# A recurrent layer on one core: the input product of two time-step pairs in seven products of halves

## The chip, the core and the metric

The kernel runs on one core of a Trainium2 chip. The core has a matrix engine (TensorE, PE in the profile), three engines for elementwise work (VectorE or DVE, ScalarE or ACT, GpSimd or POOL), and a queue engine (SyncE or SP) that issues nearly all transfers here. Each engine works through its own instructions in order and waits on semaphores for the others. Working memory is SBUF (128 partitions); TensorE writes into eight banks of PSUM, each 128 x 512 float32. The metric is the device time of one execution in microseconds, here the median of three runs.

## The reference, cut to what matters

The input x has 64 sequences of 256 time steps of 1024 numbers. Layer 0 is a recurrence:

```python
xW = jnp.einsum('ntd,dh->nth', x, Wx) + b
def step(prev_h, xw):
    next_h = jnp.tanh(prev_h @ Wh + xw)
    return next_h, next_h
_, h_t = jax.lax.scan(step, h0, swapaxes(xW, 0, 1))
x = x + swapaxes(h_t, 0, 1)
```

Layer 1 splits its input into sums and differences over time, multiplies all of them by one gate per sequence and channel, and puts them together again. Since the gate is the same for all of them, this is a multiplication of x by the gate, and with the residual x becomes x * (2 + gate) in all (the kernel's `factor`). The gate is sigmoid(silu(cond W1' + b1) W2' + b2).

So there are two large products: x Wx, which depends on nothing, over 16384 rows; and h Wh, 256 times one after the other with 64 rows.

## The kernel before

**Layout.** Two time steps are a pair (S = 2): 2 x 64 = 128 rows, which fill the array. There are NP = 128 pairs. A slab is a tile of 128 x 1024 float32, for a pair the transposed x.

**The product x Wx.** The precision wanted is that of float32[...]. Wx is split once into three parts, `wx_s[k][0..2]` (high bits, rest times 4096, and a mix of both), and so is x of each pair (class `XWork`): `high_bits` masks (L125, VectorE), `low` makes x1 = x - high (L302, VectorE), `difference` makes x2 (L307, VectorE), `cast` makes x0 (L313, ACT). `whole` then issues 48 matmuls of 128 x 128 by 128 x 512: 16 of x2 into two banks `mixed`, 16 of x1 and 16 of x0 into two banks `main` (L278). `take_mixed` takes `mixed` to SBUF (L323, ACT) and adds the bias (L324, GpSimd); `finish_half` adds `main` (L380, VectorE). The sum goes to DRAM (`store`, L390) and comes back in the layout of the h steps (`reload`, L403, eight transfers of 64 KB).

**The product h Wh.** It is a Strassen product in seven products of quarters: `StrassenWeight` holds the combinations of Wh, `strassen_sides` makes those of h (L229 to L232, four operations of 128 x 128 on VectorE, both inputs in SBUF), and `strassen_product` issues 16 small matmuls for each (L199). In the main loop the order of a step is 1, 4, 2, 5, 6, 7, 3. The quarters of the next h come off as soon as their products are there: an addition, tanh on ACT (L760), a transpose on VectorE (L764). `m5` and `m7` share the banks `main0` and `main1` with the x products.

**Stages.** The first ALONE = 12 steps run beside the loading and splitting of Wx, the gate's products and the x products of pairs 1 to 6. From step 12 on, the order on VectorE, ACT, GpSimd and SP is the program's (a manual schedule), as it is on TensorE all along. Steps come in groups of M = 2. After the second step of a group, `beside_x` issues the 48 matmuls of one pair, and around these, in this order on the other engines: the residual x + h (L623, VectorE), the scaling of finished steps by `factor` (`scale`, L505, GpSimd), the taking of `mixed`, the copies of the next step's xw into PSUM (`put_part`, L618, ACT), the split of the next pair, and the two finishes. These matmuls are what TensorE does while the last chain of the step (addition, tanh, transposes, sides) runs. I call this stretch a gap. Its sum is stored in the next group.

The outputs of the first steps, which came before `factor` was known, wait in DRAM (`kept`) and are scaled one per two gaps in `kept_step` (L732, GpSimd).

The additions of a step that matter below, in their order on VectorE:

```python
nc.vector.tensor_add(y[:, 3], m5, xw[:, 3])         # L786
transpose(0)
nc.vector.tensor_add(y[:, 3], y[:, 3], u)           # L799, u copied by ACT in L798
nc.vector.tensor_add(y[:, 2], accs[2], u)           # L800
for o in (3, 2):
    nc.vector.tensor_add(quad(h, o), m7, y[:, o])   # L804
```

## Time and profile before

| | us |
|---|---|
| median of three runs | 3045.84 (3045.01 to 3046.71) |
| the profiled execution, its own time | 3044.8 |
| its span, first to last instruction | 3043.0 |
| TensorE busy | 3033.8 |
| VectorE busy | 1797.0 |
| ScalarE busy | 871.0 |
| GpSimd busy | 844.4 |

300.59 MB were moved, 99 GB/s in the mean; the main queue took 27.5% of the 16 DMA engines' time. TensorE's granted clock was full throughout.

The profile is of one execution. Busy times are sums over an engine's instructions; since matmuls are pipelined and their ends modelled, a busy TensorE is one that had always an instruction under way. A line of the groups tells the line of the code, the engine and operation, the tiles out<-in, the shape, the count, then the busy time and the mean of one in ns, then the engine's idle time before such instructions and what ended it. The chain is followed back from the last instruction through what released each piece of work. A line of the timeline gives start, length, engine, line, and in brackets the idle time before.

### The profile page before, as it was taken

How to read it: one execution, taken by the hardware profiler on the slowest of the kernel's cores; microseconds unless marked ns; L12 is line 12 of the kernel's file. 1: busy time of each engine (PE TensorE's matmuls, PEld its weight loads, DVE VectorE, ACT ScalarE, POOL GpSimd, SP SyncE). 2: the span in 40 equal slices, each digit the busy share in tenths (PEclk: the TensorE clock that was granted, in tenths of full speed). 3: DMA queues.
4: the chain of work that ended last, by engine and by line, in shares of the span. 5: the costliest groups of instructions: out<-in, count | busy, mean ns of one | idle time of the engine just before them, and what ended most of it. 6: DMA issues, size and time to landing. Idle time of an engine off the chain costs nothing.

```text
span 3043.0 us, 144709 instructions
## 1 busy us (share of the span) xinstructions
PE 3033.8 (100%) x63862; PEld 2706.8 (89%) x63862; DVE 1797.0 (59%) x4928; ACT 871.0 (29%) x2641; POOL 844.4 (28%) x521
## 2 busy tenths in 40 slices
PE   9999999999999999999999999999999999999999
PEld 6888899889988898889888998899889988998888
DVE  8556555655555555555555565555655565565555
ACT  3222222222222222222222322232222222222222
POOL 2233333332223222322232223222222222222321
PEclk9999999999999999999999999999999999999999
DMA  7323323332222222222222222222222222222222
GB/s 264 123 90 115 101 100 100 109 107 86 86 101 98 86 86 99 100 86 86 96 99 89 86 93 97 95 86 89 102 95 86 86 102 97 86 86 102 97 86 76
DMA packets 164616, 300.59 MB, mean 99 GB/s; under 512 B 44192, under 2 KB 110496, under 8 KB 164000
## 3 DMA queue, kind: packets, MB, share of 16 engines
q1 hardware_dynamic: 163856, 290.81, 27.5%
q8 instruction: 514, 8.42, 1.1%
q14 instruction: 102, 0.84, 0.1%
q10 hardware_dynamic: 144, 0.52, 0.0%
HBM read 154.93 MB, written 136.31 MB: 96 GB/s over the span
## 4 chain that ended last, share of the span: by engine, by line
PE 98%; DMA 1%; POOL 0%; issue 0%; DVE 0%; SPq 0%; DVEq 0%; ACT 0%
PE main L278 30%; PE acc L199 22%; PE mixed L278 16%; PE m_h L199 15%; PE main_h L199 14%; PE m L199 1%; DMA h0T<-condT 0%; DMA wh<-wh 0%; DMA w<-w1T 0%; POOL sum L324 0%; PE gate_ps L216 0%; DMA x<-xT 0%; DMA b_row<-b 0%; DVE x L302 0%; SPq L134 0%
## 5 line engine op out<-in xcount | busy, mean ns | idle before, releaser
L278 PE MATMUL main<-wx,x 128*128 128x512 f32 x4064 | 945.7, 389 | 0.3 <-DVE x L302 0.3
L505 POOL TENSOR_TENSOR x<-x,factor 128x512 f32<-128x512 f32 x242 | 358.4, 1481 | 2030.8 <-issue 1177.2
L278 PEld LDWEIGHTS main<-wx,x 128*128 128x128 f32 x4064 | 762.0, 188 | 161.2 <-issue 2.2
L278 PE MATMUL mixed<-wx,x 128*128 128x512 f32 x2032 | 499.1, 397 | 0.0
L324 POOL TENSOR_TENSOR sum<-sum,b_row 128x512 f32<-128x512 f32 x254 | 448.1, 1784 | 50.6 <-DMA w<-w1T 43.2
L278 PEld LDWEIGHTS mixed<-wx,x 128*128 128x128 f32 x2032 | 371.7, 188 | 97.9 <-issue 24.8
L760 ACT ACTIVATE h<-h 128x128 f32<-128x128 f32 x976 | 275.7, 306 | 547.8 <-DVE h L784 330.9
L302 DVE TENSOR_TENSOR x<-x,x_high 128x1024 fp32r<-128x1024 f32 x127 | 171.1, 1347 | 253.6 <-PE main L278 253.5
L764 DVE STREAM_TRANSPOSE hT<-h 128x128 f32<-128x128 f32 x972 | 298.0, 307 | 38.2 <-ACT h L760 38.1
L380 DVE SCALAR_TENSOR_TENSOR sum<-main,sum 128x512 f32<-128x512 f32 x254 | 175.6, 691 | 206.2 <-PE main L278 204.5
L199 PE MATMUL acc<-wh,s 128*32 128x128 f32 x8160 | 270.8, 273 | 1.2 <-issue 1.2
L199 PE MATMUL acc<-t,hT 128*32 128x128 f32 x8160 | 270.9, 273 | 0.7 <-issue 0.7
L199 PE MATMUL acc<-wh,hT 128*32 128x128 f32 x8160 | 269.9, 273 | 0.0
L778 ACT COPY y<-m_h 128x128 f32<-128x128 f32 x244 | 65.0, 267 | 709.7 <-PE m_h L199 694.6
L199 PE MATMUL m_h<-wh,hT 128*32 128x128 f32 x7808 | 261.4, 274 | 0.3 <-issue 0.3
L199 PE MATMUL main_h<-t,s 128*32 128x128 f32 x7808 | 259.6, 273 | 0.0
L199 PE MATMUL m_h<-t,s 128*32 128x128 f32 x7808 | 258.8, 273 | 0.1
L199 PE MATMUL main_h<-wh,s 128*32 128x128 f32 x7808 | 258.6, 273 | 0.0
L199 PEld LDWEIGHTS m_h<-wh,hT 128*32 128x32 f32 x7808 | 208.6, 110 | 44.7 <-issue 44.7
L618 ACT COPY acc<-xw 128x128 f32<-128x128 f32 x732 | 177.8, 264 | 234.3 <-DMA xw<-sum_d 165.0
L323 ACT ACTIVATE sum<-mixed 128x512 f32<-128x512 f32 x254 | 152.0, 599 | 320.9 <-PE mixed L278 320.8
L307 DVE SCALAR_TENSOR_TENSOR x<-x_high,x 128x1024 fp32r<-128x1024 f32 x127 | 190.7, 1502 | 86.9 <-PE mixed L278 86.8
(81 smaller groups left out, 2931.7 us busy)
## 6 DMA issues: line engine op xcount, KB each, us to landing
x<-xT SPq DMA_DIRECT2D x127, 512.0 KB, 4.0
sum_d<-sum SPq DMA_DIRECT2D x127, 512.0 KB, 2.9
xw<-sum_d SPq DMA_DIRECT2D x1016, 64.0 KB, 2.0
yT<-x SPq DMA_DIRECT2D x122, 512.0 KB, 2.7
wh<-wh SPq DMA_DIRECT2D x8, 512.0 KB, 10.9
w<-w1T SPq DMA_DIRECT2D x8, 512.0 KB, 8.5
w<-w2T SPq DMA_DIRECT2D x8, 512.0 KB, 4.0
wx<-wx SPq DMA_DIRECT2D x7, 512.0 KB, 8.5
```

The lines of the kernel that those rows point to most:

```text
L199: nc.tensor.matmul(out=out[q * R : (q + 1) * R], lhsT=a[:, k * R : (k + 1) * R], rhs=wh_s.sides[i][k][:, q], start=first and k == 0, stop= ...
L278: nc.tensor.matmul(out=acc[h], lhsT=v[:, k * P : (k + 1) * P], rhs=wx_s[k][which][:, h * HALF : (h + 1) * HALF], start=start and k == 0, s ...
L302: nc.vector.tensor_sub(self.x1, x, self.high)
L307: nc.vector.scalar_tensor_tensor(out=self.x2, in0=self.high, scalar=1.0 + DOWN, in1=pairs[i], op0=ALU.mult, op1=ALU.subtract)
L323: nc.scalar.activation(s, self.mixed[h], AF.Copy, scale=-1.0)
L324: nc.gpsimd.tensor_add(s, s, b_row[:, h * HALF : (h + 1) * HALF])
L380: nc.vector.scalar_tensor_tensor(out=v, in0=self.main[h], scalar=1.0 + DOWN, in1=v, op0=ALU.mult, op1=ALU.add)
L505: nc.gpsimd.tensor_mul(of_step(x, s), of_step(x, s), blocks(factor))
L618: nc.scalar.copy(part, xws[t // S][t % S][:, j])
L760: nc.scalar.activation(quad(h, j), quad(h, j), AF.Tanh)
L764: nc.vector.transpose(quad(hT, j), quad(h, j))
L778: nc.scalar.copy(y[:, 0], m16)
```

## The change

The x product of pairs 16 to 127 is done for two pairs together. The 256 rows and 1024 columns of x, and Wx, are cut into quarters, and the product of the 2 x 2 quarters is made in seven products (Winograd's form of Strassen's) in place of eight. Each of the seven, a `Product`, is 12 matmuls of the same shape: four k blocks for each of x2, x1 and x0.

- **Units and chunks.** Two pairs are a unit; U = 4 units (eight pairs) are a chunk, and there are 13 of these, then one of 3 units and one of 1. Inside a chunk the products go by form (1, 2, 5, 6, 3, 7, 4), and for each form over the units.
- **Forms of Wx.** For each of the seven forms, the three parts of 128 x 2048 are made on chip and kept in DRAM (`forms_d`). Forms 1, 2 and 3 are pieces of `wx_s` and are stored during steps 2 to 10 (36 transfers of 256 KB). Forms 4 to 7 are combinations, made by `form_jobs` (GpSimd, VectorE, ACT) while the pairs 7 to 15 are multiplied in the old way, one right after another. Then the memory of the whole Wx is given up. In the main loop the three parts of a form (3 x 1 MB) are streamed in by `load_weights`, two forms ahead.
- **Forms of x.** `Form` splits a quarter of x, or a combination of quarters: a21 + a22 on VectorE for form 5, and others in place on GpSimd. These GpSimd operations, and those that add products up (`u` and `v`), are not issued where they arise but put on a list (`pool_later`), which is worked off in the first step after the gap.
- **The gap.** `beside_x` now issues 3 or 4 products (2 or 3 in the first chunk) instead of 48 matmuls. The finish of the last product and the mask and x2 of a split go into the first step after the gap, behind the copy of y0; x1 and x0 of that split go behind the copy of u, ahead of L799 (`slot`).
- **Other moves.** The two scalings of the pair before, the reload of xw and the loads of x move to the first step of a group, behind `slot`. x of a pair is read again from DRAM for the residual.

```diff
+FIRST = 16
+U = 4
+UNITS = [U] * 13 + [3, 1]
+FORMS = 3
+ORDER = (1, 2, 5, 6, 3, 7, 4)
...
+        for k in range(KB):
+            top, low = slab(f"top{k}"), slab(f"low{k}")
+            nc.sync.dma_start(out=top, in_=wx[k])
+            nc.sync.dma_start(out=low, in_=wx[KB + k])
+            l, r = cols(0), cols(1)
+            nc.gpsimd.tensor_sub(top[:, l], top[:, r], top[:, l])
+            nc.gpsimd.tensor_sub(top[:, r], low[:, r], top[:, r])
+            nc.gpsimd.tensor_sub(low[:, r], low[:, r], top[:, l])
+            nc.gpsimd.tensor_sub(low[:, l], low[:, l], low[:, r])
...
+            if self.p == 5:
+                self.src = forms.tile([P, HALF], F32, tag="s1", bufs=1, name=f"s1_{n}")
+                nc.vector.tensor_add(self.src, a[21], a[22])
+                self.later(lambda: (pool_sub(a[21], a[11], a[21]), pool_sub(a[11], a[22], a[21])))
...
+            if self.p == 6:
+                self.later(lambda: (pool_sub(a[12], a[12], a[11]), load_quarter(self.c + 1, self.v, 11)))
...
+        def first(self) -> None:
+            nc.vector.tensor_scalar(
+                out=self.high, in0=self.src[:].bitcast(I32), scalar1=HIGH, scalar2=None, op0=ALU.bitwise_and
+            )
+            nc.vector.scalar_tensor_tensor(
+                out=self.x2, in0=self.high, scalar=1.0 + DOWN, in1=self.src, op0=ALU.mult, op1=ALU.subtract
+            )
...
+        def second(self) -> None:
+            nc.vector.tensor_sub(self.x1, self.src, self.high)
+            nc.scalar.copy(self.x0, self.high)
...
+            one(self.mixed, f.x2, 2, True, True)
+            one(self.main, f.x1, 1, True, False)
+            one(self.main, f.x0, 0, False, True)
...
+            nc.scalar.activation(t, self.mixed, AF.Copy, scale=-1.0)
+            nc.gpsimd.tensor_add(t, t, add)
...
+            nc.vector.scalar_tensor_tensor(out=out, in0=self.main, scalar=1.0 + DOWN, in1=t, op0=ALU.mult, op1=ALU.add)
...
+            if p in (6, 7):
+                v = self.state("v")
+                when_h(self.c, lambda: (nc.gpsimd.tensor_add if p == 6 else nc.gpsimd.tensor_sub)(u, u, v))
...
         strassen_product(m16, sides[1], 1, True)
         nc.scalar.copy(y[:, 0], m16)
-        if t == first and coming is not None:
-            coming.cast()
+        if slot:
+            slot.pop(0)()
+        if s == 0 and i > ALONE // S and i - 1 in pairs and i < NP - 1:
+            scale(pairs[i - 1], 0)
+            scale(pairs[i - 1], 1)
+        if s == 0:
+            for f in pool_later:
+                f()
+            pool_later.clear()
+            if i + 1 < NP:
+                reload(i + 1)
+                load_x(i + 1)
...
         strassen_product(m16, sides[6], 6)
-        mark = nc.scalar.copy(u, m16)
+        nc.scalar.copy(u, m16)
+        if slot:
+            slot.pop(0)()
         nc.vector.tensor_add(y[:, 3], y[:, 3], u)
```

`beside_x` after the change:

```python
for j in range(n):
    m = done[0]
    u = Product(m, (n - 1 - j) % 2 ^ 1)
    u.multiply(n > 2 and j == n - 1)
    done[0] += 1
    if j == 0:
        residual(t, hT)
    if before and (before.c, before.v) == (u.c, u.v):
        before.finish()
        before = None
    u.take_mixed()
    if j == 0:
        accs[:] = [put_part(t + 1, o) for o in range(3)]
    if before:
        before.finish()
    before = u
    if last_of_product(m):
        load_weights(u.m + 2)
    if j + 1 < n:
        prepare()
slot.append(lambda: (before.finish(), prepare(True)))
```

## The prediction

> **What bounds the kernel now.** I read the busy shares first, then the chain that ended last, then the groups, then the timeline of one period of 23.47 us, and last the timeline of a stretch where VectorE and GpSimd meet. The page:

> ```profile
> span 3043.0 us, 144709 instructions
> PE 3033.8 (100%) x63862; PEld 2706.8 (89%) x63862; DVE 1797.0 (59%) x4928; ACT 871.0 (29%) x2641; POOL 844.4 (28%) x521
> PE 98%; DMA 1%; POOL 0%; issue 0%; DVE 0%; SPq 0%; DVEq 0%; ACT 0%
> ...
> L278 PE MATMUL main<-wx,x 128*128 128x512 f32 x4064 | 945.7, 389 | 0.3 <-DVE x L302 0.3
> L505 POOL TENSOR_TENSOR x<-x,factor 128x512 f32<-128x512 f32 x242 | 358.4, 1481 | 2030.8 <-issue 1177.2
> L324 POOL TENSOR_TENSOR sum<-sum,b_row 128x512 f32<-128x512 f32 x254 | 448.1, 1784 | 50.6 <-DMA w<-w1T 43.2
> ```

> TensorE alone sets the time; everything else is cover. The 389 ns of a matmul overlap, so its price comes from the chain in order of time:

> ```profile
> 185.05 7.25 PE main L278 x32
> ```

> 7.25/32 = 0.2266 us each. A pair costs 48 of them, 10.88 us; two h steps of 6.13 us and about 0.3 us at the seam fill up the 23.47.

> How much room do the other engines have inside a step? This is the timeline of the end of the first step of a group, which began at 1507.34 (T0 below):

> ```profile
> 1511.98 0.27 ACT L798 COPY u<-m_h 128x128 f32<-128x128 f32 x1 [0.88 <-PE m_h L199]
> 1512.28 0.29 DVE L799 TENSOR_TENSOR y<-y,u 128x128 f32<-128x128 f32 x1 [0.66 <-ACT u L798]
> 1512.49 0.28 DVE L800 TENSOR_TENSOR y<-acc,u 128x128 f32<-128x128 f32 x1
> 1512.86 0.49 DVE L804 TENSOR_TENSOR h<-main_h,y 128x128 f32<-128x128 f32 x2
> 1513.52 0.31 DVE L764 STREAM_TRANSPOSE hT<-h 128x128 f32<-128x128 f32 x1
> ...
> 1514.24 0.89 PEld L199 LDWEIGHTS acc<-t,hT 128*32 128x32 f32 x32
> ```

> The addition y3 += u (L799) starts at T0+4.94 and ends at T0+5.23; through L800, L804 and tanh it leads to the transpose that ends at 1513.83, and the second product of the next step loads that quarter at 1514.24. The slack is 0.41 us there, and 0.09 more before L804: 0.5 us. If L799 is later than that, TensorE waits.

> What can make it late is seen before the main loop (VectorE's and GpSimd's timelines):

> ```profile
> 132.35 1.38 DVE L230 TENSOR_TENSOR s<-hT 128x128 f32<-128x128 f32 x1
> 133.65 1.37 DVE L231 TENSOR_TENSOR s<-s,hT 128x128 f32<-128x128 f32 x1
> ...
> 132.18 1.39 POOL L568 TENSOR_TENSOR x<-x,hT 128x512 f32<-128x512 f32 x1 [10.56 <-DVE hT L520]
> 133.54 2.62 POOL L324 TENSOR_TENSOR sum<-sum,b_row 128x512 f32<-128x512 f32 x2
> ```

> Operations that take 0.28 us elsewhere take 1.38: each ends about 0.16 us after a GpSimd operation. The two engines take turns.

> [...] The trace agrees, with the 1.38 us above, and with L786 (one input from PSUM), which took 0.29 us at 1517.22 beside a GpSimd operation that ran from 1516.35 to 1517.64. [...] between about 4 and 26 us the DMA view shows 400 to 420 GB/s, and TensorE's matmuls waited on "issue" in four places and 1.9 us over the whole span: its instructions arrive beside full transfers.

> From these places I take as held time: 1.15 us for a GpSimd 128x512 operation (1.30 alone, less the part that overlaps), 0.55 for a VectorE two-input 128x512 one (0.69), 0.30 for the 128x512 bit mask (half of L125's 0.687, less overlap), 0.15 for a 128x128 one.

> **The change, part by part.**

> *Products removed.* Pairs 7 to 127 cost 121 x 48 = 5808 matmuls in the main part. Now pairs 7 to 15 cost 432 and 56 units of two pairs cost 56 x 7 x 12 = 4704, together 5136. 672 x 0.2266 = 152 us less. Loads of the array keep their shape (188 ns, under 226). This is the whole gain.

> *Forms of Wx (pairs 7 to 15 in a row).* The plain products hide 10.88 us of other work per pair. Every second pair loads two slabs, but their loads stand on SP behind the stores of the forms before, which wait for ACT (about 5.7 us into the pair), then 4 us landing and three GpSimd subtractions to about 15.1, then VectorE's subtraction, x1 (L302) and the first finish (L380), to about 18.3. The next pair needs that bank at 14.5. 3.8 us at pairs 10, 12 and 14 and about 0.5 at pair 8: 12 us. The 36 stores of Wx parts before that lie on SP in steps of 12.8 us with room: nothing; without room a reload of xw would be late by their 0.35 us each.

> *Hand-over.* The new pools lie on Wx's memory, so the streams start when the last plain product and its store are done (about 4 us after). The three first splits stand on VectorE and ACT before the first h step, and the second waits for a quarter of x behind 3.1 MB of weights: at the 410 GB/s of the first slice 7.7 us, plus landing. TensorE gets 3.5 us into the step, then waits for y0's copy on ACT: 12 us. Then 10.8 MB are ahead of the first reload of xw: 26 us, about 3 us beyond its cover. Together 15 us.

> *A gap.* A gap holds 3 or 4 products of 2.72 us. Per product: ACT takes mixed (0.6) and casts x0 (0.6), GpSimd adds (1.15 held), VectorE masks (0.3), makes x2 and x1 (0.55 each) and finishes (0.69, PSUM[...]). Tied by order these give a cycle of about 2.8 us, just over TensorE's 2.72. So no bank is late by more than 0.1, but the last GpSimd addition ends at about T0+1.0, and what is left runs into the step. In the gaps with two splits of a21+a22, one more addition each, a bank is 0.35 late.

> *The first step after a gap.* Here GpSimd now has two scalings of the pair before (in the kernel before they stand in the gap and beside the second step, where they meet no two-input operation on the path) and the deferred subtractions: in a chunk's eight gaps 0, 4, 5, 5, 2, 1, 3, 0 of them. VectorE has mask, x2 and x1 of a split, and then L799's y3 += u. In turns from T0+1.0: scaling to 2.15, mask 2.45, scaling 3.60, x2 4.15, deferred 5.30, x1 5.85, deferred 7.00, y3 += u 7.15, where it was 5.10. Late by 2.05, less the slack 0.5: TensorE waits 1.6 us. Without a deferred operation x1 waits only for the first transpose: 0.9 late, 0.4 us. With five, the sums of the sides collide too: 1.7. Where a21+a22 is in the split that lies in the step, 0.65 is added before and one more turn: 4.0; where two of them are in the gap, T0+1.0 becomes T0+2.3: 2.9. A chunk: 0.4 + 4.0 + 2.9 + 1.7 + 1.6 + 0.4 + 1.6 + 0.4 = 13.0, and 0.35 for the bank: 13.4. One of the three deferred operations before the seventh count and the single one before that wait for a store, so come after L799. 13 chunks: 174 us. Behind L799 on VectorE stand L800, L804 and the transposes, and TensorE waits for these.

> *Rest.* The ten scalings of the kept steps (L732) now stand ahead of the other two and shift the turns where few are deferred: 10 x 0.5 = 5. The last two chunks, with 1 to 3 products to a gap: 3. Weights (3.1 MB, 7.7 us) are asked for about 25 us ahead: nothing; the reload of xw stands behind them and behind the deferred subtractions on SP, and is in by about T0+15, the time at which the gap begins, 1.7 before its use. If that margin goes, each microsecond once per chunk costs 13. The seams stay at about 120: nothing.

> Sum on the profiled span: 3043 - 152 + 12 + 15 + 174 + 5 + 3 = 3100. The median of the runs is 2.8 above that span (3045.84 against 3043.0): 3103.

> **Rivals.**
> 1. *The turns cost less; faster or level.* The last addition may end earlier: if ACT took mixed at once, at T0+0.35, then y3 += u ends at 6.5 and the typical stall is 0.9; the chunk comes to about 7, 13 x 7 = 91 us: 3020. The break-even is (152 - 38)/13 = 8.8 us per chunk, 1.1 per gap, where 38 are the other costs with one or two more for drift. Against it: ACT's order puts the cast of x0, which waits for the mask, before the next take.
> 2. *No turns on the path; faster.* VectorE gets through between GpSimd's operations: 3043 - 152 + 35 = 2926, 2929 as a median. For it: VectorE has 41% idle time. Against it: the 1.38 us.
> 3. *The streams are the bound; slower still.* Traffic more than doubles: some 330 MB of weights, 22 of forms and 59 for reading x a second time on 300.6, or about 230 GB/s, 64% of the engines at the rate of now (99 GB/s at 27.5%). A reload late by 4 us once per chunk adds 50, and a stall in most gaps more: 3150 to 3250. Against it: 410 GB/s in the first slice.

> **How the numbers follow.** Forecast (11 to 17 us per chunk, 3070 to 3150) 0.50; rival 1 (2970 to 3060) 0.22, most of it faster; rival 2 0.12; rival 3 0.16. The time is that of the forecast. The range 2965 to 3180 holds the first two and a slice of each of the others; the forecast's own is 3070 to 3150. About 0.2% (6 us) is what this measurement tells from no change. Faster: 0.12 + 0.18 = 0.30; same 0.03; slower 0.50 + 0.16 + 0.01 = 0.67.

> **What would show it.** Right: TensorE's busy time falls by about 150, and it has new idle time of about 1.5 us before the second product of a group's second step (acc<-t,hT), released by the transpose; y3 += u takes 1.3 us in place of 0.29, so does x1's subtraction; the pattern has a period of eight gaps, worst in the second and third. One wait of 12 us or so after the ninth plain product, three near 4 us among these. Wrong: y3 += u stays at 0.3 us in the main loop, or the idle time is released by DMA, or lies between products of x. The largest risk is the place of T0+1.0: 0.5 us there moves the total by up to 50.

## The result, and the profile after

The changed kernel takes 3626.81 us (median of four runs, 3618.79 to 3629.04) against 3045.43 for the kernel before on the same chip: a ratio of 1.1905, with a 95% interval of 1.1884 to 1.1926. Slower, as forecast, but by 581 us in place of 57. The stated range ended at 3180.

The page of the kernel after, with the lines that answer to those of before (TensorE's busy sum, the chain that ended last, the costliest groups):

```profile
span 3616.7 us, 149916 instructions
PE 3092.5 (86%) x63190; PEld 2674.6 (74%) x63190; DVE 2654.7 (73%) x6017; ACT 1050.9 (29%) x3097; POOL 1387.4 (38%) x985
PE 60%; DVE 14%; issue 14%; DMA 5%; POOL 3%; ACT 2%; SPq 1%; DVEq 0%; POOLq 0%; ACTq 0%
...
L831 PE MATMUL main<-w,x 128*128 128x512 f32 x3136 | 813.1, 396 | 167.6 <-issue 161.9
L795 DVE TENSOR_SCALAR high<-a 128x512 int32<-128x512 int32 x336 | 334.1, 994 | 11.8 <-DMA a<-xT 11.7
```

TensorE was always busy before; now it idles for 14% of the span. Its busy sum, which was to fall by about 150 us, rose from 3033.8 to 3092.5, although it has 672 matmuls fewer. The chain has 14% "issue": time in which it waited for nothing that the profile shows. The mask of a split (L795) takes 994 ns in the mean for half the columns of the old one, which took 687: VectorE is held up as well.

The view of waits, TensorE's longest (engine, tile, line, what came last, then us in total, times, longest):

```profile
PE main L831 <- issue: 161.9, 106, 7.6
PE main_h L214 <- issue: 95.3, 48, 3.3
PE m_h L214 <- DVE s L247: 47.4, 21, 2.5
PE acc L214 <- DVE hT L975: 45.5, 41, 2.0
...
PE main L293 <- DVE sum L395: 26.9, 4, 8.0
...
PE m_h L214 <- ACT y L989: 12.7, 1, 12.7
```

The last three are waits that the prediction named: the second product of the second step waits for the transpose (hT), the plain products wait four times for a finish, and y0's copy comes late at the hand-over. The first two, 257 us without a releaser, it had not.

To see where the time is, I took the start of every matmul in the trace and subtracted the usual distance to the one before it (0.227 us for a product of x; the h matmuls come in regular patterns). A stall is what exceeds that by over 0.25 us.

| us, after against before | |
|---|---|
| 672 matmuls fewer | -152 |
| stalls over 0.25 us (346 of them, 597 us; before 9 us) | +588 |
| slower matmuls between the stalls | +138 |
| sum (the spans differ by 573.7) | +574 |

The slower matmuls belong to the clock for the most part: its records show 328 us at half speed after (76 intervals; one of 5 us before), and some 120 of the 138 us lie inside these. By place, the stalls of the main loop are:

| place | us | times |
|---|---|---|
| two matmuls before the end of the last product of a gap (161 us of it in the gaps of three products) | 180 | 108 |
| start of the second step of a group | 152 | 78 |
| at the last matmul of the fourth product of the second step | 98 | 46 |
| before the second product of the second step (the forecast turns) | 56 | 42 |
| hand-over, y0's copy | 13 | 1 |
| elsewhere | about 43 | |

The expectations below call the third place "at" or "before" the fourth product. Another 55 us lie before the main loop (9.5 in the kernel before), 28 of these in the four waits for a finish.

The timeline of the kernel after where a group's first step ends, TensorE's part:

```profile
1617.39 0.70 PE L831 MATMUL main<-w,x 128*128 128x512 f32 x2 [1.94 <-issue]
...
1624.94 1.04 PE L214 MATMUL acc<-wh,s 128*32 128x128 f32 x32
1628.13 1.86 PE L214 MATMUL m_h<-wh,hT 128*32 128x128 f32 x32 [2.15 <-DVE s L247]
```

The first line is the first place of the table: 1.94 us with nothing to wait for, two matmuls before the gap's end. The last is the second place. The view puts it down to a sum for the sides (L247), but that product (m_h<-wh,hT) takes hT's first quarter, transposed at 1623.95, and a bank whose copy u was in use at 1624.62. Its inputs had been there for 3.5 us.

What stands at these places? At the first, `addr_align(BLOCK, PLACE)` (L830): it fills TensorE's program with idle instructions until it stands at place 60 modulo 256. The kernel before has this too, two matmuls before its gap's end. The trace of before shows 27 idle instructions there, 1.9 us at about 72 ns each, during which TensorE works off matmuls that are already queued. The change's gaps of four products have about the same number (26 to 28), those of three have 50 to 52, which take 3.75 us: twelve matmuls fewer are 24 instructions fewer with their loads, and the padding puts 24 idle ones in their stead to reach the same place. At the other two places, counted from there (two matmuls with their loads, then 448 instructions for a step, since the trace has 32 matmuls and 32 loads for a product of h), the 452nd and the 708th instruction have passed: 196 + 256 and 196 + 512, ends of blocks of 256. The view of transfers has a queue for instructions. After:

```profile
q1 hardware_dynamic: 272288, 711.34, 56.6%
q8 instruction: 515, 8.44, 0.9%
```

### The profile page after: what moved, and what is told of

Read it like the earlier page. It is cut to its first block, busy times and chain, and to the rows that moved or that the text cites. A ratio compares the mean times of both kernels' runs of the same rounds, so it can differ in the third digit from the quotient of the medians.

```text
span 3616.7 us, 149916 instructions
## 1 busy us (share of the span) xinstructions
PE 3092.5 (86%) x63190; PEld 2674.6 (74%) x63190; DVE 2654.7 (73%) x6017; ACT 1050.9 (29%) x3097; POOL 1387.4 (38%) x985
## 3 DMA queue, kind: packets, MB, share of 16 engines
q14 instruction: 140, 1.15, 0.1%
## 4 chain that ended last, share of the span: by engine, by line
PE 60%; DVE 14%; issue 14%; DMA 5%; POOL 3%; ACT 2%; SPq 1%; DVEq 0%; POOLq 0%; ACTq 0%
PE acc L214 15%; PE main L831 14%; PE m_h L214 10%; PE main_h L214 10%; PE mixed L831 7%; DMA w<-form 3%; DVE x L807 2%; PE main L293 2%; DVE high L795 2%; DVE y L1027 2%; POOL o L860 1%; ACT h L971 1%; DVE hT L975 1%; DVE h L1032 1%; PE m L214 1%
## 5 line engine op out<-in xcount | busy, mean ns | idle before, releaser
L831 PE MATMUL main<-w,x 128*128 128x512 f32 x3136 | 813.1, 396 | 167.6 <-issue 161.9
L831 PEld LDWEIGHTS main<-w,x 128*128 128x128 f32 x3136 | 580.0, 188 | 336.2 <-issue 205.5
L860 POOL TENSOR_TENSOR o<-o,u 128x512 f32<-128x512 f32 x280 | 388.1, 1386 | 959.6 <-ACT o L859 934.0
L831 PE MATMUL mixed<-w,x 128*128 128x512 f32 x1568 | 434.6, 399 | 0.7 <-issue 0.7
L809 ACT CAST x<-high 128x512 fp32r<-128x512 f32 x392 | 243.8, 622 | 540.5 <-DVE high L795 480.7
L831 PEld LDWEIGHTS mixed<-w,x 128*128 128x128 f32 x1568 | 285.2, 188 | 77.9 <-issue 23.9
L795 DVE TENSOR_SCALAR high<-a 128x512 int32<-128x512 int32 x336 | 334.1, 994 | 11.8 <-DMA a<-xT 11.7
L800 DVE SCALAR_TENSOR_TENSOR x<-high,a 128x512 fp32r<-128x512 f32 x336 | 319.7, 951 | 29.0 <-DVE high L795 1.8
L520 POOL TENSOR_TENSOR x<-x,factor 128x512 f32<-128x512 f32 x242 | 328.7, 1380 | 10.6 <-DVE x L644 5.7
L214 PEld LDWEIGHTS m_h<-t,s 128*32 128x32 f32 x7808 | 227.4, 114 | 125.1 <-issue 101.6
L214 PEld LDWEIGHTS acc<-t,hT 128*32 128x32 f32 x8160 | 258.4, 121 | 69.9 <-DVE hT L975 57.4
```

What stands on the lines that cost most here:

```text
L214: nc.tensor.matmul(out=out[q * R : (q + 1) * R], lhsT=a[:, k * R : (k + 1) * R], rhs=wh_s.sides[i][k][:, q], start=first and k == 0, stop= ...
L520: nc.gpsimd.tensor_mul(of_step(x, s), of_step(x, s), blocks(factor))
L795: nc.vector.tensor_scalar(out=self.high, in0=self.src[:].bitcast(I32), scalar1=HIGH, scalar2=None, op0=ALU.bitwise_and)
L800: nc.vector.scalar_tensor_tensor(out=self.x2, in0=self.high, scalar=1.0 + DOWN, in1=self.src, op0=ALU.mult, op1=ALU.subtract)
L809: nc.scalar.copy(self.x0, self.high)
L831: nc.tensor.matmul(out=out, lhsT=x[:, k * P : (k + 1) * P], rhs=w[j][:, cols(k)], start=start and k == 0, stop=stop and k == KB - 1,)
```

## Theories

- **A, late pages.** The streams of weights stand in front of the pages of instructions. A page that arrives late stops TensorE at its boundary.
- **B, turns.** What the prediction said: VectorE and GpSimd take turns, the last addition is late.
- **C, late data.** The streams themselves arrive late, and TensorE waits for them inside the products of x.
- **D, padding.** The idle instructions of a gap of three products take longer than what TensorE has queued.

These letters are used in the expectations. Two of these, those on the padding, have the two kinds of gap the wrong way round: in the trace the 50 to 52 idle instructions stand in the gaps of three products. C is not borne out by the trace: no wait of TensorE in the changed kernel is put down to a part of a form, though the chain that ended last gives these parts 3%. A stall of one kind can hide another, since each makes the rest of the chain late too.

## Four runs: one cause taken away at a time, and all three

```diff
 # streams off: two forms of weights are loaded, later products use these
-        if m < 7 * len(UNITS):
+        if 2 <= m < 7 * len(UNITS):
+            weights[m] = weights[m - 2]
+        elif m < 2:
             weights[m] = {}
...
 # padding off
-            u.multiply(n > 2 and j == n - 1)
+            u.multiply(False)
...
 # GpSimd's scalings, deferred subtractions and additions off
-        nc.gpsimd.tensor_sub(out, a, b)
+        pass
...
-                when_h(self.c, lambda: (nc.gpsimd.tensor_add if p == 6 else nc.gpsimd.tensor_sub)(u, u, v))
+                pass
...
-            scale(pairs[i - 1], 0)
-            scale(pairs[i - 1], 1)
+            pass
```

> The weights of the first two products are used for all later ones; the 103 later streams (3.1 MB each) are left out, everything else is as in the changed kernel. Changed kernel: 3627 us. Theory A (TensorE's instructions, which come by DMA in pages of 16 KB, arrive late behind the 8 KB rows of the streams): the stalls of 2.1 to 3.0 us at the start of a group's second step and at its fourth product (152 and 98 us in the trace of after, of which some 40 are VectorE's) go, and with them part of the half-speed clock: 3627 - 210 - 30 = about 3390. Theory B (the turns of VectorE and GpSimd make nearly all of the loss): unchanged within 30 us, 3600 to 3627. Theory C (the streams themselves come late): the stall sits inside products, and goes too; told from A by the place of what disappears.

> The alignment before the last two matmuls of a gap is left out of the new products. In the trace of after 26 to 28 empty instructions (gaps of 3 products) or 50 to 52 (gaps of 4) stand there, at 72 ns each in TensorE's sequencer, and TensorE idles 0.4 or 2.1 us. Theory D (the padding costs what the idle time there shows): about 150 us less, 3475, unless pages of instructions now end at worse places. Theory A adds: without the alignment the page ends wander through the steps, so the stalls elsewhere spread and may grow; a gain under 80 us would say so. Theory B: no change but these 150.

> GpSimd's work in the first step after a gap is left out: the two scalings and the deferred subtractions and additions (their loads stay). Theory B (turns): the prediction's 174 us go, 3450, and y3 += u takes 0.29 us again. Theory A: what the turns cost is the 56 us before the second product of the second step and some 40 before its first, with their clock: 3500 to 3540.

> All three of these together: no streams after the second, no padding, no GpSimd work in the first step. If these are the causes, what is left is the matmuls and the two starting stretches: 3043 - 152 + 30 (forms) + 30 (hand-over, last plain product's padding of 14 us) = about 2950, up to 3000 with seams. If it stays above 3100, a further cause is open.

| taken away | us | against 3627 |
|---|---|---|
| streams | 3421.58 | -205 |
| padding | 3501.41 | -125 |
| GpSimd's work | 3605.54 | -21 |
| all three | 3106.32 | -520 |

A and D are borne out (the two executions without streams lie 40 us apart, so the 205 is good to some 20). The turns seem to cost 21 us, a seventh of the forecast, and the three differences give 351 of the 520: they cover one another. Without GpSimd's work the stalls at the start of the second step grew from 152 to 176 us: TensorE came to the page boundary earlier and waited there. With all three away 3106 is left, still 60 above the kernel before.

## The turns alone, and the padding alone

The turns can be priced only where nothing stands in front of them: streams and padding off, GpSimd's work kept.

> The changed kernel without the streams of weights after the first two forms (all later products use one of these, so their values are not the reference's) and without the padding; GpSimd's scalings and deferred operations stay. Beside the kernel with all three taken out (3106) the difference is the price of the turns when nothing else stands in front of them. Theory of the prediction (13.4 us per chunk): 3106 + 174 = 3280. Rival, from the 52 stalls of 1.3 us before the second product that the kernel without streams shows (68 us): about 3180.

Measured: 3249.29, 143 above the run without all three. The waits of that run:

```profile
PE acc L214 <- DVE hT L977: 104.6, 77, 2.3
```

The wait that was forecast (transpose, second product of the second step), 77 times, at 1.4 us each. The turns came close to the forecast: 143 in place of 174.

The padding, split between two places in place of removed (both kernels have 5027 idle instructions in all):

```diff
-            u.multiply(n > 2 and j == n - 1)
+            u.multiply({n - 1: PLACE, n - 2: FIRST_PLACE}.get(j) if n > 2 else None)
...
-                        nc.tensor.addr_align(BLOCK, PLACE)
+                        nc.tensor.addr_align(BLOCK, aligned)
...
+FIRST_PLACE = 24
```

> The changed kernel with the padding in two places, in the last product but one and in the last, so that neither takes more than about 28 places (it took 50 to 52 in gaps of four products). Theory of the padding (TensorE's sequencer passes 72 ns on each, and 1.9 us of that is hidden by matmuls that it has already queued): the 180 us at that place go, less what moves on to the next place: 3450 to 3510. Rival (TensorE waits there for a page of instructions, not for the padding): 3600 to 3630.

Measured: 3506.65, 120 less than the changed kernel. The stalls at the padding fell from 180 to 22 us (five in the first chunk, where one padding is still 121 to 127 long); some came back at the pages (start of the second step 152 to 182, fourth product 98 to 124). D is shown: the work, the page boundaries in the steps and the number of idle instructions are the same, and only how many of them stand in one place differs.

## Pages late, in the kernel before

If A holds, the kernel before must suffer as well when data move at the wrong time. I gave it copies from DRAM to DRAM that nothing reads, in the gap behind the reload.

```diff
         if later:
             xws[later.i] = later.reload(d, True)
+        if later:
+            for j in range(3):
+                spare = dram.tile([P, 2 * D], F32, tag="copied%d" % j, bufs=1, name=f"copied{later.i}_{j}")
+                src = wx[0:2].rearrange("k (p two) d -> (k p) (two d)", two=2)
+                for c in range(0, 2 * D, 2048):
+                    nc.sync.dma_start(out=spare[:, c : c + 2048], in_=src[:, c : c + 2048])
```

The second of the two runs has 512 in place of 2048, so four pieces for each copy.

> The kernel before, and beside each pair three copies of 1 MB from DRAM to DRAM in rows of 8 KB that nothing reads; all else is as it was, the padding of about 27 places too. Theory of the instruction pages (TensorE's instructions come in pages of 256 over the same DMA engines, and a page that is asked for while long rows are queued comes late): TensorE stalls by 2 to 3 us at the start of the second step and before its fourth product, as in the changed kernel: 3046 + 110 pairs x about 2.3 = 3300. Rival (the stalls belong to the new order of the work, traffic alone is harmless): 3060 at most.

> The same bytes in rows of 2 KB (twelve copies of 256 KB per pair). If it is the length of the rows that holds a page up, most of the loss of the run with rows of 8 KB is gone: under 3110. If it is the bytes: within 20 us of that run.

Measured: 3499.18 and 3486.27. The waits of the first of the two:

```profile
PE acc L199 <- issue: 286.7, 123, 4.5
```

No operation of the change is in this kernel, and it loses 454 us: 115 stalls of 2.6 us at the start of the second step, and the clock. The length of the rows makes no difference, so that part of my reading falls: the records show that what I had called rows of 8 KB moved as packets of 64 KB, and the pieces as packets of 2 KB, and the loss is within 13 us.

In these two runs and in the changed kernel the page of the second step is fetched later, and TensorE is late by the delay of the page less 0.3 to 0.9 us (from the records of the instruction queue and of the matmuls; medians):

| | page fetched, us after the first step's start | stall at the second step, us |
|---|---|---|
| before | 2.84 | none |
| changed kernel | 4.66 | 1.48 |
| before, 3 MB per pair | 6.25 | 2.56 |
| the same in 2 KB packets | 6.19 | 2.57 |

Over the groups of the third row the two columns go together with a correlation of 0.98. TensorE goes on 2.3 to 2.5 us after the packet starts; the packet itself takes 0.96.

Now is it the amount or the time at which it moves? One copy of 1 MB per pair, in the gap or tied to the first step:

```diff
+        first_copy = nc.scalar.copy(y[:, 0], m16)
         if t == first and coming is not None:
             coming.cast()
+        if t == first and later:
+            not_ahead_of(copy_one(), first_copy)
```

> The kernel before, and beside each pair one copy of 1 MB that nothing reads, issued in the gap behind the reload (the run with 3 MB had three of these there, which moved for some 17 us, until about 6.7 us into the first step). One copy is over before the first step begins. Theory of the pages, in its form that only transfers under way in the first step hold the page of the second step up: no stall, 3046 to 3060. Rival (it is the amount that counts): a third of the 454 us, about 3195.

> The same copy of 1 MB per pair, issued in the first step, behind the copy of y0 there. Theory of the pages: the page of the second step, which is fetched from 2.8 us after the start of the first step in the kernel before, stands behind it; a copy lasts about 4 us, so it comes some 2 to 3 us later and TensorE stalls for 1 to 2 us per pair: 3150 to 3280. Rival (the amount counts): as the run with the copy in the gap.

Measured: 3047.83 in the gap (ratio 1.0002, interval 0.9992 to 1.0012) and 3292.47 in the first step (1.0807, interval 1.0671 to 1.0944). The same bytes cost nothing or 245 us. By the transfers' records the copy in the gap moves from 3.6 us before the first step to 1.1 us into it, so it is over before the page is fetched (at 2.86, as in the kernel before); the other moves from 2.8 to 6.7 us. This pair of runs settles it. One group of the second, in the timeline of TensorE, then the view of transfers for 1609.3 to 1613.0 and for 1613.0 to 1614.5:

```profile
1607.23 1.08 PE L199 MATMUL m_h<-wh,hT 128*32 128x128 f32 x32
...
1612.49 1.05 PE L199 MATMUL acc<-wh,s 128*32 128x128 f32 x31
1615.49 0.27 PE L199 MATMUL acc<-wh,s 128*32 128x128 f32 x1 [1.95 <-issue]
```

```profile
q1 hardware_dynamic: 16, 1.05, 81.5%
...
q8 instruction: 1, 0.02, 4.0%
```

The copy is sixteen packets of 64 KB, all under way together, from 1610.3 to 1613.8. The page starts at 1613.52, which is to 0.01 us the end of one of these packets; 1.97 us later TensorE goes on, with the last matmul of the step, alone on the other side of the boundary. The 31 matmuls ahead of it belong to the same product and read the same tiles, so it did not wait for data. The other pages of this run look the same: of the 116 that start within 0.3 us of the end of such a packet, 72 start within 4 ns of it, where about one in eight would by chance. So most of these waited for a packet to end. With 2 KB packets, of about 0.09 us each (an estimate: 62.8% of 16 engines' 3477 us over 371216 packets), the page was as late (6.19 us after the first step's start, 6.25 with packets of 64 KB), so there it stood behind many; how many no run here shows.

## Pacing the streams

Theory A names a cure: ask for the parts of a form one at a time, in the gap, where TensorE's instructions last longer (0.227 us a matmul of x, against 6.13 us for the 224 of a step). The padding is in two places as before.

```diff
-            for j in (2, 1, 0):
-                w = weights[m][j] = stream.tile([P, KB * HALF], F32R, tag=f"w{j}", name=f"w{j}_{m}")
-                nc.sync.dma_start(out=w[:].bitcast(F32), in_=forms_d[ORDER[m % 7]][j])
+            pieces.extend((m, j) for j in (2, 1, 0))
...
         before = None
+        if pieces and n:
+            load_piece(mark)          # mark: the copy of u in the second step
...
                 load_weights(u.m + 2)
+            if pieces and j + 1 < n:
+                load_piece(u.taken)   # taken: ACT's copy of this product's mixed
```

> The changed kernel with the padding in two places (3507), and the three parts of a form asked for one at a time: one after the copy of u in the second step of a group, one after each product of the gap but the last, so that they move while TensorE works on products of x and not in the first step. Same bytes, same products. Theory of the pages: the stalls at the start of the second step and before its fourth product (182 and 124 us) go for the most part, and some of the half-speed clock: 3200 to 3290. Rival (the bytes count): 3450 or more.

Measured: 3364.10, 143 less than with the padding alone mended, so it helps as A says, and stays 74 above the upper end. Of the waits of this run:

```profile
PE acc L215 <- DVE hT L997: 59.4, 60, 2.0
...
PE main L843 <- DMA w<-form: 22.8, 25, 3.5
PE mixed L843 <- DMA w<-form: 17.6, 5, 4.7
```

The fourth product's stalls fell from 124 to 27 us, those at the start of the second step only from 182 to 123, the page being fetched at 4.58 us where it was 5.48. And pieces now come late themselves, 40 us. Nor did pacing empty the first step: in its first 3 us the DMA engines are busy for 85% of the time by the transfers' records, where it was 65% with the padding alone mended and 4% in the kernel before (means over 105 groups).

What else moves in the first step are the reload, the loads of x and the store of y, which the change put there. Four runs looked at the rest. Two without streams and GpSimd's work, to close the sum (both leave these parts of the computation out):

> The changed kernel without streams after the first two forms and without GpSimd's scalings and deferred operations (both leave part of the computation out), with the padding in two places. Without any padding the same took 3106, with some 85 us of stalls at wandering places. Theory of the pages: these are page boundaries that drift over the steps; with the padding they stand where a page has time: 3020 to 3050. Rival (the pages are late wherever the boundary stands): 3080 to 3120.

> The run before, and the transfers that the change moved into the first step (reload of xw, loads of x and of its quarters) and the store of y stand in the gap, behind the copy of u of the second step; the reload is then one pair ahead. Theory of the pages: no page is late any more, what is left is the stretch of nine plain products, the hand-over and the removed products: 2950 to 2985. Rival (a cause not yet named): above 3010.

Measured: 3111.20 and 3062.40. The first falls to the rival: the boundary is fixed again and the pages are late all the same, by a little (median 3.74 us). The second, where reload, quarters of x and y's store move into the gap, gains 49 and has the page at 3.20 us. But this kernel has a flaw: x of a pair was loaded twice, once still in the first step. So 3062 is too high by an unknown amount, and "above 3010" can't be held against A.

In it TensorE stalls 148 us (of over 0.25): 27 in the four waits for a finish, 14 and 22 at long paddings ahead of and in the first chunk, 15 at the hand-over, 25 at the fourth product, and 45 scattered. With the 152 us of removed products and 31 of slower matmuls the sum is 3043 - 152 + 148 - 9 + 31 = 3061, where its span is 3060; so nothing but these stalls and slow matmuls stands in the way of the gain; the scattered ones were not followed up.

The same with the streams, nothing left out (the first text again with the double load; the second with one load; the last two with y3 += u from PSUM and the split's x1 in the second step):

> The paced kernel (3364) with the same transfers taken out of the first step; nothing is left out. Theory of the pages: the 123 us at the start of the second step and the 27 at its fourth product shrink to a third, the turns show instead (some 100 to 140 us): 3190 to 3270. Rival (the second step starts late because its inputs are late): 3330 or more.

> The paced kernel with the moved transfers in the gap, as in the run at 3474, but x of a pair loaded once. Theory of the pages: against the paced kernel (3364) the stalls at the start of the second step shrink, and the gap has room for 5.3 MB at about 400 GB/s: 3230 to 3320. Rival (the gap is full, and what is taken out of the first step makes the pieces late and runs on into the next step): 3350 to 3450.

> The same, and y3 += u takes u from PSUM, and x1 and x0 of the split that stands in the first step are made in the second, behind the copy of y0 there; nothing is left out. Theory (the turns are what is left): 2990 to 3090, so level with the kernel before or faster. Rival (the streams still cost, as 5.3 MB per pair fill all of the gap): 3150 or more.

> The same with y3 += u from PSUM and the split's x1 and x0 in the second step. Against the run before it the turns' share: the pair at 3474 and 3408 differ by 66, so 50 to 90 us less than e17. If it comes under 3046, the seven products pay after all; the theory of a full gap says 3290 to 3380.

| | us |
|---|---|
| paced (from above) | 3364.10 |
| moved transfers in the gap too, x twice | 3473.60 |
| the same, x once | 3419.84 |
| with the two edits against the turns, x twice | 3407.53 |
| the same, x once | 3369.62 |

The rival of a full gap holds. The waits of the run at 3420:

```profile
PE acc L215 <- DVE hT L1026: 73.2, 59, 2.0
PE main L859 <- DMA w<-form: 64.7, 25, 4.5
...
PE mixed L859 <- DMA w<-form: 18.4, 5, 4.7
```

Waits for weights went from 40 to 83 us, and the page of the second step was not earlier (4.47 after 4.58): what was taken out of the first step runs on into it from the gap. The DMA engines are busy for 94% of the gap (76% with pacing alone) and for 95% of the first step's first 3 us (85%). The double load (63 MB, one of the two in the first step) cost 54 and 38 us. No order that I tried has room for these streams, the pages and the rest.

## An addition from PSUM

To test B itself, y3 += u reads the product in PSUM in place of its copy in SBUF (streams and padding off, against 3249).

```diff
-        nc.vector.tensor_add(y[:, 3], y[:, 3], u)
+        nc.vector.tensor_add(y[:, 3], m16, y[:, 3])
```

> The run without streams and padding (3249), and y3 += u reads the product m16 in PSUM in place of its copy u in SBUF, the same values; later products use weights of other forms, as there. Theory of the turns (an addition with two inputs in SBUF waits for the end of GpSimd's operation): the last turn goes, and most of the 143 us between 3249 and 3106 with it: 3130 to 3170. Rival (the addition is late because of the split's operations ahead of it on VectorE): 3215 to 3250.

Measured: 3196.87, between the two. The waits tell why:

```profile
PE m_h L214 <- DVE y L1029: 61.3, 49, 2.9
...
PE acc L214 <- DVE hT L977: 0.7, 2, 0.4
```

TensorE's waits for the transpose before the second product fell from 104.6 us to 0.7, as the turns say. But the addition still stands behind the split's x1 on VectorE, and now it holds the bank m16, which the next step's first product needs: 61 us there. So the turn of the addition is real, and so are those of the operations ahead of it.

## Why the prediction was wrong

**Products removed, -152: right.** The matmuls come at the same distances, and the sum closes with 152.

**Turns, +174: right in the mechanism, 31 too much, and mostly covered.** The price alone is 143; in the changed kernel taking them away gave 21. In the run with the turns alone, the stalls from the start of the second step to its second product, a mean over twelve chunks, gap by gap:

| gap of the chunk | 1 | 2 | 3 | 4 | 5 | 6 | 7 | 8 | sum |
|---|---|---|---|---|---|---|---|---|---|
| forecast, us | 0.4 | 4.0 | 2.9 | 1.7 | 1.6 | 0.4 | 1.6 | 0.4 | 13.0 |
| measured, us | 0.04 | 4.20 | 2.62 | 1.69 | 1.22 | 0.59 | 1.37 | 0.57 | 12.3 |

Thirteen such chunks are 160; the run without all three has some 15 us at these places too, and 160 - 15 is the 143 within 2. The instruction-by-instruction working holds within 0.4 us for each gap. In the changed kernel the mask (L795) takes 0.43 us with no GpSimd operation beside it and 0.95 beside one (medians), at most 1.54; the finish, which reads PSUM (L868), takes 0.68 to 0.69 in both cases. A first step in the changed kernel (VectorE, GpSimd and TensorE in the timeline):

```profile
1545.46 6.16 POOL L770 TENSOR_TENSOR a<-a,a 128x512 f32<-128x512 f32 x4
1548.28 0.86 DVE L807 TENSOR_TENSOR x<-s,high 128x512 fp32r<-128x512 f32 x1
1549.07 1.35 DVE L1027 TENSOR_TENSOR y<-y,u 128x128 f32<-128x128 f32 x1
...
1551.57 1.08 PE L214 MATMUL acc<-t,hT 128*32 128x128 f32 x32 [1.98 <-DVE hT L975]
```

The addition takes 1.35 us in place of 0.29 beside four deferred subtractions, and TensorE waits 1.98, as worked out. In the changed kernel 44 of 122 first steps have it over 0.6 us, in the run with the turns alone 73: elsewhere TensorE was late already, so that u came after GpSimd had done.

**Streams, "nothing": the step that failed.** The prediction priced a stream by what waits for its data and left out what waits behind it. It even looked at the right thing, and took from the start of the kernel that "its instructions arrive beside full transfers". That stretch did not show it: the pages of the kernel before are fetched there at 14.1, 22.0 and 27.9 us, one in 6 to 8 us, while an h step needs one every 3.5 us. In the trace 250 us of stalls stand at page boundaries (16.5 of these end with u's copy, L1024, and 14.7 of that kind remain without the streams); without the streams the time is 205 less.

**Padding: not in the sum.** L830 stood in the code with the same call as before, and the trace of before showed the idle instructions, covered. Their number depends on what lies between two such places, and it nearly doubled in gaps of three products: 180 us at the place, 120 to 125 in time.

**Clock: not in the sum.** In the kernel before stalls came to 9 us in all, and the granted clock was full but for 5 us at the end. TensorE now idles again and again for 2 us or more and is slowed after: of the 76 half-speed intervals 75 begin in a stall of over 2 us or within 3.5 us of its end (the other stands at the kernel's end), and none follows shorter stalls alone. The slower matmuls are 138 us, the largest term that no single edit owns. Not every such stall is followed by an interval (3.4 us or multiples of it): 61 of the 143 between 2 and 3.2 us were, and 14 of the 15 longer ones. In the kernel before with 3 MB per pair there are 74 intervals.

**Forms stretch, +12: right in the place, too low.** Pairs 8, 10, 12 and 14 wait 4.5, 7.4, 8.2 and 7.4 us where 0.5 and three times 3.8 were given: 28, and 14 more for 248 idle instructions ahead of the last plain pair's end. Why each is late by 4 us more was not tried.

**Hand-over, +15: right.** 13 at y0's copy. **Gap cycle: right.** A bank is late 17 times, 8 us in all.

**Rivals.** The third (3150 to 3250, 0.16) had the right part of the machine, with a reload as the thing that is late. It did come late (VectorE waits for xw 19 times, 56.5 us in all), but TensorE's long stalls lie at pages and padding. Rivals 1 and 2, turns at 91 us or none, are excluded by the 143, and even with streams, padding and GpSimd's work gone the kernel takes 3106. Of the signs of being wrong, idle time between products of x came nearest: 180 us lie inside the last product of a gap.

## What to carry to other kernels

A transfer has a price for whoever stands behind it on the engines, here TensorE with its own program (1 MB per pair cost 0.4 us in the gap, 245 in the first step): look in the trace for the queue of instructions, count which instruction opens each page, and see that no bulk transfer is under way when the next page is asked for. That the transfer was asked for in the stretch before is not enough: look where it ends. Padding that sets the place of a boundary must be counted again after every edit (twelve matmuls fewer took it from 26 to 28 idle instructions to 50 to 52), and put where enough queued work covers it (27 of them, 1.9 us, were covered). A stall that is taken away alone may show little (the turns 21 us, and 143 with the others gone); price it with the others gone, and count the clock with the idle time (138 us of slower matmuls here).

## What the hardware showed that I had not expected

1 MB per pair costs 0.4 us in the gap, which is no change, and 245 us in the first step. A copy of 1 MB between contiguous DRAM tiles moves as sixteen packets of 64 KB of some 3 us each, and a page of instructions starts at the end of one of them; packets of 2 KB hold it up by as much (454 and 441 us for 3 MB per pair). In TensorE's program 27 idle instructions at the end of a gap cost nothing in the kernel before; in the changed kernel 26 to 28 cost 0.4 us and 50 to 52 cost 2.2 us (medians). Stalls of some 2 to 3 us were followed by the half clock in 61 of 143 cases there, and in 32 of 65 with the copy of 1 MB in the first step. The seven products did not pay in any order tried: the fastest version with nothing left out, the paced one, takes 3364 us, 7% less than the changed kernel and 10% more than the kernel before. What the streams cost at the least, if the gap had room, stays open.
